# A memset of one unread column behind each gather on GpSimd (four graph layers on a sparse adjacency)

## The chip, the cores and the metric

The kernel runs on one core of a Trainium2 chip. The metric is device time in microseconds of one execution, as the median of three timed runs. A profile is one more execution of the same program with the hardware profiler on; its times are shown beside the timed runs and are not the same thing.

## What is computed

Four layers run one after the other on 4096 nodes with 128 features. Each normalises its input, applies ReLU, and adds the layer's result to its input. The adjacency matrix `adj` (4096 x 4096, float32) is mostly zeros, and the share of non-zeros falls from the first nodes to the last.

```python
h = relu(layernorm(x));  x = x + h @ W_self.T + (adj @ h) @ W_neigh.T + b          # layer 0
h = relu(layernorm(x));  T1 = adj @ h;  T2 = 2 * (adj @ T1) - h                     # layer 1
x = x + h @ w[0] + T1 @ w[1] + T2 @ w[2] + bias
h = relu(layernorm(x));  H = h @ weight.T                                           # layer 2: attention
C = (H * att_src).sum(-1)[None, :] + (H * att_dst).sum(-1)[:, None]
Tau = adj.T * exp(maximum(0.2 * C, C))
x = x + (adj.T * Tau / Tau.sum(1, keepdims=True)) @ H
h = relu(layernorm(x));  s = h @ msg_s;  d = h @ msg_d                              # layer 3: messages
agg[i] = sum_j gelu(s[i] + d[j] + msg_b) * adj[i, j]
x = x + layernorm(gelu(concat(h, agg) @ upd.T + upd_b) + h) * ln_w + ln_b
```

## The kernel before

**Dense part and lists.** The nodes are reordered on the host so that the well-connected ones come first. Products with `adj` are done in stripes of 256 rows or columns (`ROWS`, `COLS`). For each stripe the near blocks of 128 nodes (the first ones and its own) are read and multiplied whole. For the rest the kernel makes a list on the chip of the (node, stripe) pairs that hold a non-zero, and fetches only those: a piece of 256 values of `adj` and the node's feature row, 128 list entries in one gather. For layer 3 it makes a list of the single non-zero entries (`entries`), with their column numbers (`e_col`), addresses (`e_at`) and values (`e_val`). If a list should overflow, a branch at the end runs a dense fallback (`dense_stack`); it is not run with these inputs.

**The gathers.** Every gather goes through one helper, `gather`, at line 552: an indirect DMA issued by GpSimd that takes 128 row numbers from a column in SBUF and fetches these rows of a table in DRAM. It is called from six places:

- `Layer.gather`: for layers 0 to 2 of the products (layer 1 is two of them), the pieces of `adjT` (`rseg`, only in the first product, from where SP stores them to `r_tab` for the later ones) and the feature rows (`g` from `h_tab` and `u_tab`)
- `fetch_columns`: the pieces of `adj` by column (`cseg`), which SP stores to `c_tab` for the attention layer
- `Attention.rows`: rows of `a_tab` (`g`)
- `values`: the values `e_val`, 4 bytes for each partition
- `Messages.rows`: rows of `d_tab`, into the message buffers (`m`, and later the halves of the attention buffers, which the trace calls `tau` and `e`)

**The order.** A planner (`Plan`) runs when the program is built. Each piece of work is a generator that yields what it wants next: an event, a buffer, or an engine for some time. The planner takes them in order of the time at which they could begin and of their rank, and so writes out one fixed order of instructions for each engine; `in_order` then pins it. A gather is booked as `GATHER`, 1.27 us of GpSimd (`"POOL", 1.27`), and its data as landing 4 us after the transfer. The planner also puts matmuls of zeros (`fill`, line 610) into gaps of TensorE. Instructions that are issued without a `yield` cost nothing in the plan.

**What waits for what.** Buffers set the pace between the engines: 14 tiles `g` for feature rows, 6 `cseg`, 8 `rseg`, 4 messages at first and more later. A gather waits until the buffer's last reader is done (PE for `g`, SP's store for `rseg` and `cseg`), and PE waits until the gathered rows have landed. Dependencies between engines are semaphores: each engine has its own count, and DMAs from GpSimd and from SP have eight counts each, used in turn. GpSimd's other work is small: the constants at the start, and the bias additions at lines 980 and 1001.

Of the kernel before, what the change touches and what calls it, by code (L numbers as in the profile page):

```python
# [27 lines left out]
P = 128  # L28
# [350 lines left out]
def sparse_stack(tc, x, adj, adjT, diag, w_self, w_neigh, b0, w1, b1, w2, att_src, att_dst,  # L379
# [7 lines left out]
    nc = tc.nc  # L387
    plan = Plan()
    EARLY = 7
    with ExitStack() as ctx:  # L390
# [4 lines left out]
        def tiles(pool, name, n, shape, dtype=F32):  # L395
            return Slots([pool.tile(list(shape), dtype, name=f"{name}{i}", tag=f"{name}{i}") for i in range(n)])

        def kept(name, shape, dtype=F32):
            return keep.tile(list(shape), dtype, name=name, tag=name)
# [149 lines left out]
        junks = tiles(keep, "junk", 2, (P, D))  # L549
        aggs = tiles(keep, "agg", 2, (P, BANK))  # L550

        def gather(dst, table, index):
            nc.gpsimd.indirect_dma_start(out=dst, out_offset=None, in_=table[:, :],  # L553
                                         in_offset=bass.IndirectOffsetOnAxis(ap=index, axis=0))


        def norm(blocks, dst):
# [174 lines left out]
        def fetch_columns():  # L732
            for s in COLS:
                if s.cap:
                    yield col_list[s.index]
                for k in range(s.cap):
                    t = yield csegs
                    yield GATHER
                    gather(t, adj_segments, seg_col[:, s.chunk + k:s.chunk + k + 1])
                    here, left = Event(), Count(1)  # L740
                    here.set(plan.transfer(P * CS * 4))
                    plan.start(store(here, t, csegs, left, c_tab[s.index][k * P:(k + 1) * P, :], c_done[s.index],
                                     P * CS * 4), 6)
                    plan.start(give_back(left, csegs, t), 0)
# [186 lines left out]
        def values():  # L931
            for number, group in enumerate(GROUPS):
                yield decoded[number]
                for u in group.units:
                    for k in range(u.chunk, u.chunk + u.cap):
                        yield GATHER
                        n = u.within(k)
                        gather(e_val[:n, k:k + 1], adj_flat, e_at[:n, k:k + 1])
                        valued[u.number].set(plan.finish + plan.LANDING)
                    plan.start(valid(u), 7)  # L940
# [125 lines left out]
        class Layer:  # L1066
# [36 lines left out]
            def gather(self):  # L1103
                for s in ROWS:
                    if s.cap:
                        yield row_list[s.index]
                    for c in range(s.cap):
                        if self.number == 0:
                            t = yield rsegs
                            yield GATHER  # L1110
                            gather(t, adjT_segments, seg_row[:, s.chunk + c:s.chunk + c + 1])
                            here, left = Event(), Count(2)
                            here.set(plan.transfer(P * RS * 4))
                            self.at["seg", s.index, c] = t, here, left
                            plan.start(store(here, t, rsegs, left, r_tab[s.index][c * P:(c + 1) * P, :],
                                             r_done[s.index], P * RS * 4), 2)
                            plan.start(give_back(left, rsegs, t), 0)
                        g = yield rows_g
                        yield self.table_done
                        yield GATHER  # L1120
                        gather(g[:, :D], self.table, fetch_row[:, s.chunk + c:s.chunk + c + 1])
                        self.at["row", s.index, c] = g
                        self.rows_here[s.index][c].set(plan.transfer(P * D * 4))
# [538 lines left out]
def gnn_stack_kernel(tc, **args):  # L1662


    some_bad = sparse_stack(tc, **args)
    with tc.If(some_bad > 0):
        args.pop("diag")
        dense_stack(tc, **args)
# [329 lines left out]
```

## Time and profile before

| | before |
|---|---|
| median of three timed runs | 1174.64 us (1171.81 to 1176.21) |
| the profiled execution, its own time | 1485.49 us |
| its span | 1483.4 us |
| mean granted TensorE clock in it | 0.842 |
| gathers, all from line 553 | 736 |
| GpSimd busy with them | 727.74 us |
| traffic of SP's DMA queue | 186.45 MB |
| traffic of GpSimd's DMA queue | 48.27 MB |

The profiled execution took 311 us longer than the median of the timed runs. In the page and its views, PE is TensorE's matmuls, PEld its weight loads, DVE is VectorE, ACT ScalarE, POOL GpSimd and SP SyncE; an engine with a q behind it is that engine's sequencer, where DMAs are issued. A row of the timeline is: start in us from the span's start, duration in us, engine, line, operation, what it writes and reads, how many instructions are merged, and in brackets how long the engine had been idle and what ended that. "remote" and "another core or an unknown queue" mean that a semaphore was raised by something for which the profile has no matching instruction; "issue" means that the engine waited for nothing that the profile shows. A row of the waits is: engine, what waited, its line, what it waited for, and then total us, how often, and the longest.

Where the gathers lie, from the stretches of the profile (us from the start of the span):

| stretch | gathers | mean DMA share | what runs |
|---|---|---|---|
| 0 to 85 | 1 | 0.90 | first reading of `adj`, constants |
| 85 to 375 | 132 | 0.86 | rest of the reading, layer 0 |
| 375 to 900 | 304 | 0.54 | two products of layer 1, lists and values |
| 900 to 1200 | 164 | 0.34 | attention |
| 1200 to 1430 | 136 | 0.21 | messages |
| 1430 to 1484 | 2 | 0.09 | last blocks |

### The profile page before, as it was taken

What the parts mean: (1) busy time and instruction counts of PE and PEld (TensorE: products, weight loads), DVE (VectorE), ACT (ScalarE), POOL (GpSimd) and SP (SyncE); (2) the same over time, 40 slices, a digit from 0 to 9 for tenths busy, and PEclk for the clock granted to TensorE, in tenths of its full rate; (3) what the DMA queues carried; (4) which work ended last, traced back from release to release, by engine and by line L of the source; (5) the groups of instructions that cost most, each with busy time, mean ns of one, the idle gap of its engine ahead of it and who ended that gap; (6) DMA issues with size and microseconds to landing.
All of it is one profiled execution on the core that took longest, in us unless ns stands there. A gap on an engine that the chain in (4) does not pass through costs nothing.

```text
span 1483.4 us, 19188 instructions
## 1 busy us (share of the span) xinstructions
PE 1055.1 (71%) x5943; PEld 722.2 (49%) x5943; DVE 792.7 (53%) x2982; ACT 671.2 (45%) x1344; POOL 766.4 (52%) x832
## 2 busy tenths in 40 slices
PE   6786778877486687667677069968767872957774
PEld 2454556554265465455555045534434452645663
DVE  5796567787466476345645048444444451424453
ACT  5983466664021213113335048656555630334366
POOL 4136664344635565546656733765557346664530
PEclk9897799897697899778888579979888995988988
DMA  8999899895565777766544034333333212112210
GB/s 252 357 329 334 286 299 330 305 353 185 135 185 147 211 228 227 201 187 181 150 115 132 8 93 132 107 88 89 88 107 97 61 50 49 42 42 53 61 45 24
DMA packets 175415, 236.03 MB, mean 159 GB/s; under 512 B 22452, under 2 KB 155336, under 8 KB 167112
## 3 DMA queue, kind: packets, MB, share of 16 engines
q1 hardware_dynamic: 148904, 186.45, 37.8%
q0 software_dynamic: 26400, 48.27, 13.6%
q8 instruction: 49, 0.80, 0.2%
q14 instruction: 62, 0.51, 0.1%
HBM read 203.41 MB, written 31.23 MB: 158 GB/s over the span
## 4 chain that ended last, share of the span: by engine, by line
PE 23%; another core or an unknown queue 13%; ACT 10%; DVE 7%; issue 6%; DMA 1%; POOL 0%; ACTq 0%; SPq 0%; DVEq 0%; POOLq 0%
PE acc L1253 4%; PE acc L1255 3%; PE bank L597 2%; PE acc L1421 2%; PE acc L1139 2%; PE acc L1156 2%; ACT junk L1453 1%; ACT e L1229 1%; ACT junk L568 1%; PE bank L1411 1%; PE pick L610 1%; ACT e L1232 1%; PE bank L1409 1%; DVE ehit L891 1%
## 5 line engine op out<-in xcount | busy, mean ns | idle before, releaser
L553 POOL DMA_INDIRECT e_val<-in_adj,e_at x158 | 154.5, 978 | 48.0 <-issue 45.6
L553 POOL DMA_INDIRECT g<-h_tab,fetch_row x136 | 136.1, 1001 | 73.0 <-issue 34.3
L610 PE MATMUL pick<-nothing 128*128 128x512 f16 x536 | 142.9, 416 | 1.6 <-issue 1.6
L1139 PE MATMUL acc<-big,hA 128*128 128x256 f32 x448 | 131.7, 442 | 10.7 <-issue 7.7
L610 PEld LDWEIGHTS <-nothing 128*128 128x128 f16 x795 | 82.9, 107 | 99.3 <-issue 33.4
L553 POOL DMA_INDIRECT g<-a_tab,fetch_col x74 | 76.9, 1039 | 93.6 <-issue 45.3
L553 POOL DMA_INDIRECT rseg<-in_adjT,seg_row x68 | 71.1, 1046 | 103.4 <-issue 28.8
L1139 PEld LDWEIGHTS acc<-big,hA 128*128 128x128 f32 x448 | 96.4, 225 | 28.6 <-issue 9.5
L553 POOL DMA_INDIRECT cseg<-in_adj,seg_col x74 | 70.8, 957 | 63.9 <-issue 23.2
L891 DVE SCALAR_TENSOR_TENSOR ehit<-ehit,pos,pick 128x32 f32<-128x32 f32 (+7 forms) x158 | 38.8, 285 | 116.0 <-issue 80.1
L1236 DVE TENSOR_TENSOR tau<-e,big 128x512 f32<-128x512 f32 (+3 forms) x61 | 54.3, 891 | 85.5 <-ACT e L1232 47.8
L553 POOL DMA_INDIRECT g<-u_tab,fetch_row x68 | 64.6, 950 | 64.9 <-PE acc L1156 37.1
L888 ACT COPY ehit<-pick 128x192 f32<-128x192 f32 (+7 forms) x74 | 20.4, 286 | 154.5 <-remote 80.4
L553 POOL DMA_INDIRECT tau<-d_tab,e_col x63 | 60.6, 962 | 57.2 <-issue 15.0
L769 ACT ACTIVATE mask<-dst 128x2048 fp8e4<-128x2048 f32 x43 | 81.8, 1903 | 14.2 <-DMA dst<-in_adj 8.0
L553 POOL DMA_INDIRECT m<-d_tab,e_col x70 | 68.4, 977 | 38.5 <-issue 17.4
L1156 PE MATMUL acc<-big,g 128*128 128x256 f32 x272 | 80.2, 434 | 0.6 <-DMA big<-r_tab 0.5
L568 ACT ACTIVATE junk<-xN,stat 128x128 f32<-128x128 f32 x128 | 51.4, 401 | 60.0 <-DVE stat L564 27.0
L623 ACT ACTIVATE sel_t<-iota_row,mids 128x512 f32<-128x512 f32 (+3 forms) x43 | 27.1, 642 | 109.7 <-DVE mids L618 63.7
L610 PE MATMUL bank<-nothing 128*128 128x512 f16 x259 | 70.6, 414 | 2.7 <-issue 2.3
L884 PE MATMUL pick<-eA,esel 128*128 128x65 f16 (+7 forms) x158 | 27.0, 245 | 61.4 <-DVE esel L625 28.0
L1139 PE MATMUL acc<-big,hB 128*128 128x256 f32 x224 | 62.7, 420 | 1.7 <-DMA big<-in_adjT 1.7
(331 smaller groups left out, 2717.2 us busy)
## 6 DMA issues: line engine op xcount, KB each, us to landing
dst<-in_adj SPq DMA_DIRECT2D x43, 1024.0 KB
big<-in_adjT SPq DMA_DIRECT2D x45, 512.0 KB
raw<-in_adj SPq DMA_DIRECT2D x21, 1024.0 KB
big<-in_adjT SPq DMA_DIRECT2D x66, 256.0 KB
big<-r_tab SPq DMA_DIRECT2D x30, 512.0 KB
c_tab<-cseg SPq DMA_DIRECT2D x74, 128.0 KB
r_tab<-rseg SPq DMA_DIRECT2D x68, 128.0 KB
big<-c_tab SPq DMA_DIRECT2D x15, 512.0 KB
```

What stands on the lines that cost most here:

```text
L553: nc.gpsimd.indirect_dma_start(out=dst, out_offset=None, in_=table[:, :], in_offset=bass.IndirectOffsetOnAxis(ap=index, axis=0))
L568: nc.scalar.activation(junk, src[:, k, :], AF.Square, bias=st[:, 0, k:k + 1], accum_out=st[:, 1, k:k + 1])
L597: nc.tensor.matmul(p[:, k * D:(k + 1) * D], lhs[:, k * P:(k + 1) * P], w, start=i == 0, stop=i == len(terms) - 1)
L610: nc.tensor.matmul(idle[2][idle[1]], nothing[:, :P], nothing, start=True, stop=True)
L769: nc.scalar.activation(mask[:, h * HALF:(h + 1) * HALF], raw_of[b, h], AF.Sigmoid, scale=1e38, accum_out=marks[:, 2 * b + h:2 * b + h + 1] ...
L891: nc.vector.scalar_tensor_tensor(hit[:, q, :], hit[:, q, :], pos0[:, k + q:k + q + 1], pv[:, q, W:2 * W], op0=ALU.is_le, op1=ALU.mult, acc ...
L1139: nc.tensor.matmul(acc, self.near[:, b, :D], as_rows(t)[:, k, :], start=count == 0, stop=count == every - 1)
L1156: nc.tensor.matmul(acc, row[:, :D], r, start=count == 0, stop=count == every - 1)
L1236: nc.vector.tensor_mul(tau[:, :n, :], e[:, :n, :], a[:, :n, :])
L1253: nc.tensor.matmul(acc[0:1, CS:2 * CS], parts[k][:, D + 1:], tau[:, k, :], start=False, stop=False)
L1255: nc.tensor.matmul(acc[:, :CS], parts[k][:, :D], e[:, k, :], start=False, stop=self.count[s.index] == every - 1)
L1421: nc.tensor.matmul(acc[:, b % GB * P:(b % GB + 1) * P], m[:, q, :], r[:, q, :], start=False, stop=all(self.left[g * GB + k] == 0 for k in ...
```

## The change

A tile of one column, 128 x 1 float32, is added, and `gather` writes zeros into it with a memset on GpSimd after each indirect DMA. Nothing reads this tile. The planner's booking of a gather is left as it is.

```diff
+        spacer = kept("spacer", (P, 1))
+
         def gather(dst, table, index):
+
             nc.gpsimd.indirect_dma_start(out=dst, out_offset=None, in_=table[:, :],
                                          in_offset=bass.IndirectOffsetOnAxis(ap=index, axis=0))
+            nc.gpsimd.memset(spacer, 0.0)
```

In the built program this is 736 memsets, each directly behind a gather on GpSimd's queue, and each with a wait on GpSimd's own count for the memset before it, since both write the same column.

## The prediction

> **What bounds the kernel now.** I read the times beside the page first, then the chain that ended last, then the waits of GpSimd, then stretches of the timeline in order of time.
>
> The first thing to see is that the profiled execution took 1485.49 us and the three timed ones have a median of 1174.64 us. So 311 us of the profile have no counterpart in the timed runs, and I have to find them before I use it. The page and its chain of waits:
>
> ```profile
> span 1483.4 us, 19188 instructions
> PE 1055.1 (71%) x5943; PEld 722.2 (49%) x5943; DVE 792.7 (53%) x2982; ACT 671.2 (45%) x1344; POOL 766.4 (52%) x832
> ...
> PE 23%; another core or an unknown queue 13%; ACT 10%; DVE 7%; issue 6%; DMA 1%; POOL 0%; ACTq 0%; SPq 0%; DVEq 0%; POOLq 0%
> ```
>
> No engine is full. 13% (13.4% by line, 199 us) of the chain is a wait with no visible releaser and 6.4% (95 us) is "issue". The long pieces are all of one kind. The timeline at the largest of them:
>
> ```profile
> 828.10 0.17 ACT L1042 ACTIVATE hB<-bank 128x2 f32<-128x2 f32 x1 [15.11 <-remote]
> 828.31 0.16 DVE L1044 COPY hB<-bank 128x2 f32<-128x2 f32 x1 [4.12 <-issue]
> ...
> 853.79 0.94 POOL L553 DMA_INDIRECT e_val<-in_adj,e_at  x1 [0.30 <-issue]
> 855.04 0.93 POOL L553 DMA_INDIRECT e_val<-in_adj,e_at  x1 [0.30 <-issue]
> 855.43 0.24 ACT L888 COPY ehit<-pick 128x96 f32<-128x96 f32 x1 [27.16 <-remote]
> 855.71 0.25 DVE L891 SCALAR_TENSOR_TENSOR ehit<-ehit,pos,pick 128x32 f32<-128x32 f32 x1 [26.91 <-issue]
> ```
>
> ACT waits 27.16 us for matmuls that, earlier in the timeline, started by 815.7 us. While every other engine stands still, GpSimd goes on gathering with 0.94 us busy and a 0.30 us gap. A similar wait of 32.43 us ends at 1258.5, again inside an unbroken run of gathers. Those two shares make 294 us, almost the 311 us that the timed runs do not have. My reading is that these standstills come mostly with being profiled, and that the timed runs are a program without them.
>
> What bounds that program is suggested by GpSimd's own waits:
>
> ```profile
> POOL g L553 <- issue: 93.7, 215, 28.9
> POOL g L553 <- PE acc L1156: 60.5, 20, 14.2
> ...
> POOL e_val L553 <- issue: 45.6, 150, 0.3
> POOL rseg L553 <- issue: 28.8, 47, 8.5
> POOL cseg L553 <- issue: 23.2, 65, 1.2
> ```
>
> Columns are total, times, longest. Adding m (57), tau (49) and e (19), 602 of the 736 gathers (82%) have no named releaser, mostly the plain 0.30 us: they follow another gather at once. A gather holds GpSimd for 1.25 us from start to start, not for its 0.94, so 736 of them are 920 us. Before 85 us there are none and after 1430 us two. Outside stand 85 + 54 = 139 us; if the timed run keeps those, 1175 - 139 = 1036 us are left for 920 us of gathers: 89% full. PE, DVE and ACT are below that in total. So GpSimd is close to the bound in the timed run, though the profile puts it at 52% and its share of the chain at 0%. The 89% is an upper reading: if profiling also stretches the gather itself, it is less.
>
> [...] The trace agrees that busy times mislead here: 128x1 memsets of 0.10 us start 0.03 us apart. [...]
>
> **The change part by part.** It removes nothing. It adds 736 memsets of 128x1, one behind each gather on GpSimd's queue, and one 4-byte column per partition. Set side by side, the two instruction streams differ in nothing else: outside the fallback branch PE, DVE, ACT and SP have the same instructions and waits in the same order, and no DMA is added or passes another. The planner doesn't know of the memset (it still books 1.27 us per gather).
>
> The memset carries one wait, on GpSimd's own count, for the memset before it (both write the same column). That one was issued a whole gather, 1.25 us, earlier and shows as 0.10 us long, so the wait should always be met. Queued behind it are the next gather and, eight times at line 1001, a bias addition; what waits for those is PE (gathered rows), SP (stores of segments) and DVE (values). Eight existing instructions lose a wait on the same count because the memset in front already covers it; I cost that at nothing.
>
> The price of one memset, from the trace:
>
> ```profile
> 0.28 0.10 POOL L1986 MEMSET const-float32-1.0<- 128x1 f32 x1
> ...
> 3.57 1.54 POOL L474 MEMSET unit_base<- 128x26 f32 x32
> 5.04 0.75 POOL L403 DMA_DIRECT2D b_sb<-in_b  x1
> ```
>
> 32 narrow memsets take from 3.57 to 5.04 us, so 0.046 us each. For the neighbours of a gather, the nearest rows are a bias addition between two gathers:
>
> ```profile
> 163.14 0.94 POOL L553 DMA_INDIRECT rseg<-in_adjT,seg_row  x1 [0.30 <-issue]
> 164.09 1.28 POOL L1001 TENSOR_TENSOR xN<-xN,b_sb 128x512 f32<-128x512 f32 x1
> 165.53 0.96 POOL L553 DMA_INDIRECT g<-h_tab,fetch_row  x1 [0.16 <-issue]
> ```
>
> It starts 0.01 us after the gather ends, and the gap before the next gather is 0.16 instead of 0.30: 0.14 us of its 1.28 overlap with the start of the gather. By this row a 0.10 us memset could cost nothing. Bounds: 0 below (all hidden), 0.10 us above (its whole busy time, nothing overlapped), and 0.26 us if 0.10 plus a 0.16 gap came on top of the 0.30. Below nothing only by the first rival. I take 0.046: 736 x 0.046 = 34 us of GpSimd's time.
>
> What of this lies on the path? None where DMA sets the pace: from 85 to 375 us DMA is 0.86 busy and 132 gathers x 1.25 fill 165 of 290 us, 57%. That leaves 604 gathers, 28 us. Of those I count most but not all, since GpSimd also sits behind PE (the 60.5 us above), which absorbs some. I take 24 us, 70% of the 34. The sum on the profile's own execution: 1485 + 24 = 1509 us; the standstills can move this by far more than 24 either way. Against the timed median: 1174.6 + 24 = 1199, forecast 1198.
>
> **The rivals.**
>
> Faster: the spacer breaks the standstills. Place: the unbroken runs of gathers, 801 to 857 and 1208 to 1253 us above all. For it: engines stand still exactly there, and a short instruction that is no gather may let the others through. Against it: the 311 us leave room for almost none of them in the timed run, and each gather already leaves 0.30 us. Price: if a third of the 199 us (66) exists unprofiled and all of it goes, less the 24, the gain is 42: 1132 us. It decides the sign once more than 24 us of real standstill is cured.
>
> No change: GpSimd has slack. For it: 0% of the chain and waits behind PE. It needs less than 6 us of the 34 on the path, under 18%: 1176 us. Against it: 82% of the gathers follow a gather.
>
> Much slower: the memset does not overlap. At 0.10 us, 74 us on GpSimd, 70% on the path 52: 1226 us. At 0.26, 191 and 134: 1308 us, which the 0.16 gap after the addition speaks against.
>
> **How the numbers follow.** Forecast 0.47 (its own range 1182 to 1215), faster rival 0.28, no change 0.12, much slower 0.13. A measurement of this kernel can tell about 0.5%, 6 us. So faster 0.28, same 0.12, slower 0.60. The range to hold 8 in 10 takes in the forecast, the no-change case, the part of the faster case that stops at 1132, and the 0.10 us case: 1132 to 1240. Left out are larger cures (0.13) and the 0.26 end (0.05).
>
> **What would show it.** GpSimd's start-to-start time of two gathers with a memset between them: 1.25 + 0.05 us is my step, 1.25 the no-change row, 1.35 or more the costly rival. The memset's idle before it should be about nothing; an idle that names GpSimd itself would prove the wait on its own count wrong. The wait with no named releaser should stay near 13% of the chain if the memset does not touch the standstills. If it shrinks to a few per cent and the timed median falls with it, the standstills were real and my reading of the 311 us is wrong; if it shrinks in the profile while the time rises, the reading holds and only the profile was cured. A time below 1169 us proves the forecast wrong outright.

## The result, and the profile after

The change makes the kernel slower by half a per cent: 1183.54 us (median of 19 runs, 1175.28 to 1187.99) against 1175.98 us for before (19 runs in the same comparison), ratio 1.0052, 95% interval 1.0035 to 1.0069. As a share of 1176 us that is about 6 us, 4 to 8 by the interval. The forecast was 24 us.

One thing has to be known to read the numbers: in some places (chips, or occasions: the record does not tell these apart) this program takes about 1176 us whether or not it is changed, and in others, profiled or not, 1477 to 1521 us, so each ratio is between runs of one comparison on one chip, with their slow executions left out, and is not the quotient of the two medians.

The page of the changed kernel, its first part, the chain of waits and, from the costliest groups, two of GpSimd's (busy us, mean ns of one, then idle time of the engine before them):

```profile
span 1184.9 us, 19920 instructions
PE 984.4 (83%) x5943; PEld 673.4 (57%) x5943; DVE 792.3 (67%) x2982; ACT 672.6 (57%) x1344; POOL 865.8 (73%) x1568
...
POOL 27%; PE 21%; DMA 19%; DVE 14%; ACT 11%; issue 7%; POOLq 0%; SPq 0%; DVEq 0%; ACTq 0%
...
L556 POOL DMA_INDIRECT e_val<-in_adj,e_at x158 | 158.9, 1006 | 30.0 <-issue 28.4
...
L558 POOL MEMSET spacer<- 128x1 f32 x736 | 94.6, 129 | 0.3
```

The instruction count is up by 732 (736 memsets, and four other records fewer), and PE, DVE and ACT have the counts of before. The chain now adds up to about 100% and has no wait without a releaser; GpSimd leads it with 27%. The 736 memsets show 94.6 us of busy time, but hardly any idle in front of them (0.3 us in all).

The next view is GpSimd's timeline in an unbroken row of gathers:

```profile
690.07 0.94 POOL L556 DMA_INDIRECT e_val<-in_adj,e_at  x1 [0.19 <-issue]
691.01 0.12 POOL L558 MEMSET spacer<- 128x1 f32 x1
691.32 0.94 POOL L556 DMA_INDIRECT e_val<-in_adj,e_at  x1 [0.19 <-issue]
692.26 0.11 POOL L558 MEMSET spacer<- 128x1 f32 x1
692.57 0.95 POOL L556 DMA_INDIRECT e_val<-in_adj,e_at  x1 [0.19 <-issue]
```

A gather starts every 1.25 us, as before the change. The 0.30 us that stood empty between two gathers now hold a memset of 0.12 us and a gap of 0.19. Over all start-to-start times below 1.7 us the median is 1.249 us here and 1.249 us in the profile of before. So the memset's busy time, 94.6 us by the page, is nowhere in the queue's pace. (The profile of before comes from one of the slower places; the start-to-start time was 1.249 or 1.250 us in all of them.)

It would be easy to read a 300 us gain into the two profiles, 1483.4 us against 1184.9 us. The timed runs beside them say +0.5%. That pair of profiles compares two places more than two kernels, and the first experiments had to separate the two.

### The profile page after: what moved, and what is told of

Same layout as the page of the kernel before. It is cut to its first block, busy times and chain, and to the rows that moved or that the text cites. A ratio compares the mean times of both kernels' runs of the same rounds, so it can differ in the third digit from the quotient of the medians.

```text
span 1184.9 us, 19920 instructions
## 1 busy us (share of the span) xinstructions
PE 984.4 (83%) x5943; PEld 673.4 (57%) x5943; DVE 792.3 (67%) x2982; ACT 672.6 (57%) x1344; POOL 865.8 (73%) x1568
## 4 chain that ended last, share of the span: by engine, by line
POOL 27%; PE 21%; DMA 19%; DVE 14%; ACT 11%; issue 7%; POOLq 0%; SPq 0%; DVEq 0%; ACTq 0%
POOL e_val L556 7%; POOL g L556 6%; DMA g<-h_tab,fetch_row 4%; POOL m L556 4%; PE acc L1160 4%; POOL spacer L558 3%; PE acc L1143 3%; PE pick L614 3%; DMA dst<-in_adj 2%; PE bank L601 2%; ACT junk L572 2%; DMA cseg<-in_adj,seg_col 2%; DMA g<-a_tab,fetch_col 2%; ACT mask L773 2%; POOL cseg L556 2%
## 5 line engine op out<-in xcount | busy, mean ns | idle before, releaser
L556 POOL DMA_INDIRECT e_val<-in_adj,e_at x158 | 158.9, 1006 | 30.0 <-issue 28.4
L1143 PE MATMUL acc<-big,hA 128*128 128x256 f32 x448 | 119.5, 412 | 8.3 <-DMA big<-in_adjT 5.9
L1143 PEld LDWEIGHTS acc<-big,hA 128*128 128x128 f32 x448 | 87.8, 205 | 22.9 <-DMA big<-in_adjT 7.7
L558 POOL MEMSET spacer<- 128x1 f32 x736 | 94.6, 129 | 0.3
L556 POOL DMA_INDIRECT g<-a_tab,fetch_col x74 | 78.5, 1061 | 16.0 <-issue 10.3
L1160 PE MATMUL acc<-big,g 128*128 128x256 f32 x272 | 75.4, 411 | 11.7 <-DMA g<-h_tab,fetch_row 6.6
L1143 PE MATMUL acc<-big,hB 128*128 128x256 f32 x224 | 59.6, 402 | 11.3 <-DMA big<-in_adjT 11.1
L614 PE MATMUL bank<-nothing 128*128 128x512 f16 x259 | 66.6, 399 | 0.0
L1160 PEld LDWEIGHTS acc<-big,g 128*128 128x128 f32 x272 | 51.6, 202 | 22.7 <-DMA g<-h_tab,fetch_row 8.7
```

Source lines behind the costliest of these rows:

```text
L558: nc.gpsimd.memset(spacer, 0.0)
L614: nc.tensor.matmul(idle[2][idle[1]], nothing[:, :P], nothing, start=True, stop=True)
L1143: nc.tensor.matmul(acc, self.near[:, b, :D], as_rows(t)[:, k, :], start=count == 0, stop=count == every - 1)
L1160: nc.tensor.matmul(acc, row[:, :D], r, start=count == 0, stop=count == every - 1)
```

## The experiments

In the tables and texts, "start-to-start" is the median distance of two gathers less than 1.7 us apart, and "standstill" is the sum of all stretches over 2 us in which PE, PEld, DVE and ACT start no instruction; both are counted from the trace. Medians in the tables are over all timed runs of an experiment. Experiments on one chip were e1 to e4, e5 to e8, e9 to e12, e13 to e16, and e17 with e18; on all five, before took 1477 to 1521 us.

### Do the standstills belong to the profile, and does the change cure them?

The kernel before was run again without an edit, three times (e1, e5, e9), and the change once (e6).

> The kernel before, unchanged, profiled and timed once more. Timed ratio to before 1.000 within 0.3%. Theory 'the standstills belong to a profiled kernel without the memset': its span is near 1480 us again, with 13% of the chain without a releaser. Rival 'the standstills were an accident of that one execution': its span is near 1176 us and the median start-to-start time of back-to-back gathers is still 1.249 us, GpSimd about 80% taken.

> The kernel before, unchanged, for a profile beside the next three. Ratio 1.000 within 0.4%. Theory 'the standstills go with the place where the program runs': its timed median and its profile agree, either both near 1176 us with no standstill or both near 1485 us with them. Rival 'the standstills go with the profile': timed near 1176 us and profiled near 1485 us. In both the start-to-start time of back-to-back gathers is 1.249 us.

> The kernel before once more, for its profile beside the next three. Ratio 1.000 within 0.4%. By the runs so far timed and profiled time agree on one chip: both near 1485 us or both near 1176 us. In the second case the profile shows what the change was measured against: start-to-start 1.249 us, GpSimd's gathers nearly one unbroken row from 100 to 1140 us, no wait without a releaser.

> The change, unchanged. Where before takes about 1176 us: ratio 1.003 to 1.007 and start-to-start 1.249 us, as measured. Where before takes about 1485 us: theory 'the memset is no cure for the standstills, its queue time is hidden': ratio 1.00 to 1.02 (the own-column memsets gave 1.0127, the pairs 1.0233); rival 'it cures them': ratio below 0.97.

| run | timed median, us | ratio to before (95%) | span of its profile, us | start-to-start, us | standstill, us |
|---|---|---|---|---|---|
| e1 before | 1484.65 | 0.9981 (0.994 to 1.0021) | 1493.8 | 1.249 | 162 |
| e5 before | 1480.08 | 1.0066 (1.0021 to 1.0111) | 1471.4 | 1.250 | 158 |
| e9 before | 1507.66 | 1.0017 (0.9956 to 1.0079) | 1502.4 | 1.249 | 170 |
| e6 change | 1498.89 | 1.0139 (1.0064 to 1.0214) | 1508.6 | 1.249 | 179 |

Timed and profiled runs agree on every chip. The long times are therefore not made by the profiler, and neither, it follows, are the standstills: they come and go with the place. e5 is the same kernel as its reference and still reads 1.0066, with an interval up to 1.0111, so in these places a ratio within about 1% of 1 says nothing.

The timeline of e9, at the same work that stood still in the profile of before:

```profile
866.50 0.94 POOL L553 DMA_INDIRECT e_val<-in_adj,e_at  x1 [0.30 <-issue]
867.75 0.92 POOL L553 DMA_INDIRECT e_val<-in_adj,e_at  x1 [0.30 <-issue]
868.80 0.24 ACT L888 COPY ehit<-pick 128x96 f32<-128x96 f32 x1 [27.17 <-remote]
...
869.08 0.25 DVE L891 SCALAR_TENSOR_TENSOR ehit<-ehit,pos,pick 128x32 f32<-128x32 f32 x1 [26.92 <-issue]
```

ACT waited 27.17 us, at the same instruction and for as long as in the profile of before (27.16). The change has such waits too when it runs in such a place; from e6's timeline of ACT:

```profile
848.01 0.24 ACT L892 COPY ehit<-pick 128x96 f32<-128x96 f32 x1 [16.04 <-remote]
850.11 0.58 ACT L1169 COPY agg<-acc 128x512 f32<-128x512 f32 x1 [1.86 <-remote]
867.93 0.17 ACT L1046 ACTIVATE hB<-bank 128x2 f32<-128x2 f32 x1 [17.24 <-remote]
```

So a memset of one column cures nothing, and the calm profile of the changed kernel was taken where, by the timed 1176 us of before, there was little to cure.

The changed kernel was thus profiled in both kinds of place, and its two traces can be set side by side. In the first 85 us, with one gather, they agree: 382 matmuls in the calm trace and 375 in e6, at a granted clock of 0.92 in both. Then e6 falls behind as the gathers go on, by 10 us at the 41st, 129 us at the 361st and 302 us at the last. Standstills of over 2 us are 179 us of that in e6 and 14 us in the calm trace; so they are about half of the difference, and the rest is shorter waits and longer matmuls (PE is busy 1061 us against 984 us). The granted clock of TensorE is lower in the slow places, 0.82 to 0.85 against 0.92 to 0.94, and could be a cause of its own. In the profile of before it is 0.50 inside the standstill from 812 to 856 us and 1.00 in busy work from 900 to 940 us. Whether the lower clock adds to the time by itself or only goes along with the standstills is not shown; no run separates the two.

### Is it the wait on GpSimd's own count, or the number of memsets?

e2 gives each memset a column of its own, which takes the wait away. e3 and e10 put two memsets behind each gather.

```diff
-        spacer = kept("spacer", (P, 1))
+        spacer = kept("spacer", (P, 736), U8)
+        used = iter(range(736))
-            nc.gpsimd.memset(spacer, 0.0)
+            k = next(used)
+            nc.gpsimd.memset(spacer[:, k:k + 1], 0)
```

```diff
-        spacer = kept("spacer", (P, 1))
+        spacers = [kept(f"spacer{i}", (P, 1)) for i in range(2)]
-            nc.gpsimd.memset(spacer, 0.0)
+            for spacer in spacers:
+                nc.gpsimd.memset(spacer, 0.0)
```

> Each memset writes a column (one byte per partition) of its own, so none waits on GpSimd's own count. Theory 'the memset lies in the 0.30 us that a gather leaves anyway, and the 6 us come from something else than the wait': ratio 1.003 to 1.007, as the change. Rival 'the 6 us are the wait on its own count': ratio 1.000 within 0.2%. In both the start-to-start time stays 1.25 us.

> Two memsets of 128x1 behind each gather, on two columns. Theory 'cover': the second adds about 0.03 to 0.05 us, because 0.12 us of memset and 0.19 us of gap already fill the 0.30 us: start-to-start 1.28 to 1.30 us, ratio 1.015 to 1.03 (736 x 0.04 = 29 us, most of it on the path as GpSimd is nearly full). Rival 'the price was always 0.046 us a memset and the path takes only a fifth of it': start-to-start also up, but ratio only 1.010 (another 6 us).

> Two memsets again; start-to-start 1.25 us, as measured. Where before takes about 1176 us: theory 'each memset costs a little at places where gathers are not back to back': ratio 1.008 to 1.012, twice the change's. Rival 'the change's 0.5% has nothing to do with the number of memsets': 1.003 to 1.007. Where before takes about 1485 us: 1.015 to 1.03.

e2 came to 1.0127 (1.0085 to 1.0168) with start-to-start 1.249 us, beside 1.0139 for the change on another chip. Both ratios that I had named for it, 1.000 and 1.003 to 1.007, failed. Nothing points to the wait as the price: without it the ratio is the same, and with it the memsets of the change stand idle for 0.3 us in all. A part of a per cent could still hide in these intervals. e3 gave 1.0233 (1.0171 to 1.0294) and e10 1.012 (1.0048 to 1.0191). My expectation that the second memset would add 0.03 to 0.05 us failed: start-to-start was 1.250 and 1.249 us. For e10 I had named 1.015 to 1.03 in such a place, and it fell just short. From e3's timeline of GpSimd:

```profile
641.78 0.14 POOL L559 MEMSET spacer<- 128x1 f32 x2
642.09 0.94 POOL L556 DMA_INDIRECT g<-u_tab,fetch_row  x1 [0.16 <-issue]
643.03 0.14 POOL L559 MEMSET spacer<- 128x1 f32 x2
643.33 0.94 POOL L556 DMA_INDIRECT g<-u_tab,fetch_row  x1 [0.16 <-issue]
```

Two memsets take 0.14 us and leave a gap of 0.16, again 0.30 together. The cover is not used up by one memset, nor by two. A median hides rare cases, so here are the means of the same distances. On e6's chip it is 1.273 us with one memset and 1.273 without (e5). On e3's chip it is 1.273 with e2's memset, 1.276 with two and 1.271 without (e1). On e10's chip it is 1.279 with two and 1.266 without (e9). Profiles of the kernel before differ by 0.007 us in this mean, so one memset shows nothing in it, and two show a hint of 0.005 to 0.013 us. In e3 and e10 the memsets also waited for GpSimd's own count, for 9.6 and 9.9 us in all. Whether the number of memsets matters for the time is inconclusive: e3 says more than the change, e10 says the same. All four runs with narrow memsets in these places read 1.2 to 2.3% above before, more than the 0.5% of the main comparison. After e5's 1.0066 that is a hint and no more, and what the time would go into is not shown.

### How long must the memset be to show?

The wider memsets were meant to measure the price: for 128x128 (e4) I expected 4 to 6% more time. It came out 3% faster, and the rest of the series follows that surprise. They are otherwise the change (`kept("spacer", (P, 128))`, `(P, 192)`, `(P, 2 * P)`, and `(P, 448), F16`). e12 puts one behind every second gather only, e16 writes 256 columns of the upper 64 partitions only.

e12:

```diff
-        spacer = kept("spacer", (P, 1))
+        spacer = kept("spacer", (P, 484), F16)
+        used = iter(range(736))
-            nc.gpsimd.memset(spacer, 0.0)
+            if next(used) % 2:
+                nc.gpsimd.memset(spacer, 0.0)
```

e16:

```diff
-        spacer = kept("spacer", (P, 1))
+        spacer = kept("spacer", (P, 2 * P))
-            nc.gpsimd.memset(spacer, 0.0)
+            nc.gpsimd.memset(spacer[64:128, :], 0.0)
```

> The memset is 128x128, about 0.20 us long by the rows of the kernel before. Theory 'cover, GpSimd nearly full': 0.20 + 0.19 us of gap against 0.30, so start-to-start 1.33 to 1.36 us, 59 to 80 us more on GpSimd, ratio 1.04 to 1.06 if 80% or more of it is on the path. Rival 'GpSimd has slack, a fifth is on the path': ratio 1.010 to 1.015 with the same start-to-start time.

> The 128x128 memset again (start-to-start 1.331 us, 0.082 us more than before, 60 us in all on GpSimd). Where before takes about 1176 us: theory 'GpSimd is nearly full': ratio 1.03 to 1.05; rival 'most of it falls in slack': 1.010 or less. Where before takes about 1485 us: again 0.96 to 0.98.

> The memset is 128x192, start-to-start about 1.385 us. Theory 'a sustained rate fills something, with a limit near 1.4 us a gather': between the two neighbours, ratio 0.91 to 0.95, standstills of over 2 us adding to 30 to 110 us. Rival 'the limit lies at or under 1.38': 0.87 to 0.90, better than 128x256, since less queue time is spent. Where before takes about 1176 us: 1.06 to 1.09.

> The memset is 128x256, about 0.33 us: start-to-start 1.44 us, 0.19 us more than before, 140 us in all on GpSimd. Where before takes about 1176 us: theory 'nearly full': ratio 1.08 to 1.11; rival 'slack': 1.03 or less. Where before takes about 1485 us: if what helps is the longer pause between gathers, ratio below that of 128x128 or equal to it; if that gain was chance, above 1.00.

> The 128x256 memset, start-to-start 1.438 us, 0.189 us more than before, 139 us in all on GpSimd. Where before takes about 1176 us: theory 'GpSimd nearly full, 70% or more of its queue time is on the path': ratio 1.08 to 1.12; rival 'slack, a fifth': 1.02 to 1.03. Where before takes about 1485 us: 0.89 to 0.91 again.

> The 128x256 memset as the base for the next one. Where before takes about 1485 us or more: 0.89 to 0.905; start-to-start 1.44 us.

> A memset of 128x448 half-precision columns behind every gather, start-to-start about 1.60 us, 0.16 us more than with 128x256, 118 us in all on GpSimd. With standstills gone in both, the difference in time over 118 us is the share of GpSimd's queue time on the path. Theory 'GpSimd nearly full': 80 to 118 us slower than the 128x256 memset. Rival 'a fifth is on the path': 20 to 30 us slower.

> A memset of 128x484 half-precision columns behind every second gather only: 0.38 us more behind every second one, the mean start-to-start is that of the 128x256 memset, 1.44 us. Where before takes about 1485 us: theory 'a sustained rate of gathers fills something, only the mean pace counts': ratio 0.88 to 0.92. Rival 'each gather needs a pause of its own': 0.95 or more. Where before takes about 1176 us: as the 128x256 memset, within 1%.

> The memset writes 256 columns of partitions 64 to 127 only. Theory 'a memset is hidden where it runs beside the preparation of the next gather on other partitions': start-to-start falls back to about 1.25 us and the ratio to 1.00 to 1.02. Rival 'the next gather waits for the whole memset whatever its partitions': start-to-start 1.44 us and ratio 0.89 to 0.91, as for all 128 partitions.

| memset | runs | start-to-start, us | ratio to before (95%) | standstill, us |
|---|---|---|---|---|
| none | e1, e5, e9 | 1.249 | 1 | 158 to 170 |
| 128x128 | e4 | 1.331 | 0.9696 (0.9625 to 0.9767) | 124 |
| 128x128 | e7 | 1.331 | 0.9813 (0.9726 to 0.99) | 132 |
| 128x192 | e15 | 1.388 | 0.919, 1397.44 / 1521.25, no interval (its four runs: 1374.53 to 1408.28) | 102 |
| 128x256 | e8 | 1.438 | 0.8966 (0.8868 to 0.9063) | 19 |
| 128x256 | e11 | 1.442 | 0.898 (0.8911 to 0.9049) | 33 |
| 128x256 | e13 | 1.438 | 0.892 (0.8854 to 0.8985) | 44 |
| 64x256 | e16 | 1.438 | 0.8923 (0.8857 to 0.8989) | 46 |
| 128x484 half precision, every second | e12 | mean 1.44 (1.26 and 1.63 in turn) | 0.9053 (0.8982 to 0.9125) | 53 |
| 128x448 half precision | e14 | 1.598 | 0.9358 (0.9284 to 0.9432) | 64 |

Two readings come out of this table. The first is the price. From the timelines of GpSimd in e4 and in e14:

```profile
639.49 0.95 POOL L556 DMA_INDIRECT g<-u_tab,fetch_row  x1 [0.16 <-issue]
640.43 0.22 POOL L558 MEMSET spacer<- 128x128 f32 x1
640.82 0.95 POOL L556 DMA_INDIRECT cseg<-in_adj,seg_col  x1 [0.16 <-issue]
```

```profile
704.72 0.49 POOL L558 MEMSET spacer<- 128x448 f16 x1
705.38 0.95 POOL L556 DMA_INDIRECT e_val<-in_adj,e_at  x1 [0.16 <-issue]
706.32 0.50 POOL L558 MEMSET spacer<- 128x448 f16 x1
```

In all of these rows the gap behind the memset is 0.16 us. In them and in the rows with one or two narrow memsets (gaps of 0.19 and 0.16 us behind 0.12 and 0.14 us of memset), a gather starts 0.30 us after the last one ended, or 0.16 us after the memset between them ended, whichever is later. So up to 0.14 us of memset cost nothing in pace, 0.22 us cost 0.08 (1.331 against 1.249), and 0.50 us cost 0.35. e16 speaks against the idea that it matters which partitions the memset writes: one of partitions 64 to 127 takes 0.33 us and leads to a start-to-start of 1.438 us, as one of all 128 does in e13. The preparation of a gather that its expectation names is not seen in any trace.

The second is the share of GpSimd's time on the path. e13 and e14 ran on one chip. e14 has 0.160 us more for each of 736 gathers, 118 us, and took 1418.95 instead of 1354.29 us, 65 us more, or 55%. My expectation named 80 to 118 us for a nearly full GpSimd and 20 to 30 for the rival; it fell between them. But the two differ in more than the pace, as their chains of waits show, e13 first:

```profile
PE 25%; POOL 20%; DVE 15%; issue 12%; DMA 12%; ACT 10%; another core or an unknown queue 5%; SPq 0%; POOLq 0%; ACTq 0%; DVEq 0%
```

```profile
POOL 42%; PE 20%; DMA 15%; issue 8%; DVE 8%; ACT 6%; SPq 1%; POOLq 0%; DVEq 0%; ACTq 0%
```

e13 still has 5% of unnamed waits (4.5% by line, 61 us) and e14 has none. What e14 saved there can hide as much of its longer queue, so 55% is more likely too low than too high, and nothing up to the whole 118 us is excluded. The clock differs too (0.86 against 0.89).

The table also shows that the standstills answer to pace. They shrink step by step as the gathers are spaced out, to 19 to 53 us at 1.44 us. At 1.598 us they are not shorter (64 us in e14, 44 and 46 us in e13 and e16 on the same chip), but e14 has no wait without a named releaser any more; its longest stretch, 10.7 us, ends when gathered values land. A pause behind every second gather does nearly as well as one behind each (0.9053 against 0.898 on the same chip), so a pause for each gather is not needed, which fits that the mean pace counts. A fixed number of gathers in a row does not bring a standstill on: the ten longest of e1 begin after 5 to 33 gathers less than 1.7 us apart, and in the calm trace of the change a row of 97 passes with one such stretch, of 4 us. The end of the standstills can be read in e8's chain of waits, where the share without a releaser is 1%:

```profile
PE 29%; POOL 27%; DVE 12%; DMA 12%; issue 9%; ACT 8%; another core or an unknown queue 1%; SPq 1%; POOLq 0%; ACTq 0%; DVEq 0%
```

Beside it e9, the kernel before:

```profile
PE 42%; DVE 16%; another core or an unknown queue 14%; issue 12%; ACT 10%; DMA 3%; POOL 1%; SPq 0%; ACTq 0%; DVEq 0%; POOLq 0%
```

With the unnamed waits nearly gone, GpSimd rises from 1% to 27% of the chain (20% in e13 and 24% in e11, where some are left). That it is the same 27% as in the calm profile of the change is chance, since e8's gathers are slower and its memsets longer.

### Does TensorE's filler matter, and can more be had?

e17 is the kernel before with the line `plan.filler = fill` taken out, so the 795 matmuls of zeros and their weight loads are not issued. e18 is the 128x256 memset with the planner's booking of a gather set to it.

```diff
-            plan.filler = fill
```

```diff
-GATHER = "POOL", 1.27
+GATHER = "POOL", 1.46
```

> The kernel before without the planner's filler: the matmuls of zeros at line 610, 795 of TensorE's 5943 matmuls with as many weight loads, are left out; nothing reads their result. Theory 'what fills up is shared by the instructions of all engines and by the gathers': standstills of over 2 us fall well below the 160 to 180 us of the kernel before, ratio 0.97 or less where before takes about 1485 us or more. Rival 'it is the gathers alone': standstills stay within 150 to 190 us and the ratio is 0.99 to 1.03.

> The 128x256 memset behind each gather, and the planner books 1.46 us for a gather instead of 1.27, so the order of instructions is made for the longer gather. Theory 'the order matters because GpSimd is nearly full': 0.86 to 0.885 against before (the pause alone gave 0.892 to 0.898). Rival 'the order is the same in effect': 0.885 to 0.91.

The expectations of e12, e15 and e17 speak of something that fills up; that is a picture and no run shows such a store. e17: 1.0162 (1.0073 to 1.025), standstill 194 us, start-to-start 1.250 us. About a seventh of TensorE's instructions less does not shorten the standstills, so there is no sign that their number brings these on. The time is no clean measure here, as the mean granted clock fell to 0.777 as well. e18: 0.9076 (0.8991 to 0.9161), start-to-start 1.440 us, standstill 23 us. The order made for longer gathers is no better than the pause alone (0.892 to 0.898 on other chips).

The versions with the 128x256 memset, without the new booking, take 10 to 11% less than before in the places where before takes 1477 us or more. Where before takes 1176 us they were not tried. An estimate from the two readings above: the memsets add 0.189 us x 736 = 139 us of queue time there, and with 55% to all of it on the path they should lose some 6 to 12%.

## Why the prediction was wrong

It forecast slower, by 24 us; slower was right, the size was four times too large. The sum was 736 x 0.046 us, of which 70% on the path.

**The price of one memset: this term failed.** I took 0.046 us from 32 memsets in a row at the start of the kernel. That is what a memset costs behind another memset. Behind a gather it falls into 0.30 us in which GpSimd starts nothing, and start-to-start stayed at 1.249 us with one (the change, e6) and 1.250 us with two (e3). The row with the bias addition said so before: a gap of 0.16 us instead of 0.30, hence 0.14 us of cover. The prediction read it, listed nothing as the lower bound, and still took the other row. The nearer row was the right one, because it was between two gathers. In place of 0.046 us the runs show 0.00 us at the median, and 0.002 us or less on the mean (e6 against e5, e2 against e1).

**The share on the path** was 70%, by judgement, and is not decided: e14 against e13 gives 55% at a slower pace, more likely too low than too high. With 55% to all on the path, the 4 to 8 us measured would be 0.005 to 0.020 us a memset. The pace of back-to-back gathers does not show that, so where these 6 us come from stays open. No run points to the wait on its own count (e2).

**GpSimd is nearly full in the undisturbed program**: right in what it counted, the time taken by the queue. In the profile of the change, gathers run from 101 to 1153 us, and 736 x 1.249 = 919 of these 1052 us are theirs, 87%; 89% was forecast. It leads the chain with 27%. So the no-change rival came close in size for another reason than it gave: the cover in front of each gather was enough, and slack of GpSimd was not needed.

**The wait is always met, and nothing else moves**: right. 0.3 us idle before 736 memsets, and the other engines' counts are the same.

**"These standstills come mostly with being profiled": wrong.** Timed and profiled runs agree in e1, e5 and e9, at 1480 to 1508 us timed and 1471 to 1502 us profiled. The sum that supported it, 294 us against 311 us, was a coincidence: it added all "issue" time of the chain to the unnamed waits, while the standstills counted from that trace are 174 us, and a slower place would have fitted as well. A timed run beside the profile on the same chip would have told; by these runs, the two I compared came from different places. The sign that the prediction had set for this came out the wrong way: the unnamed waits vanished from the profile while the time rose, which was to mean that only the profile had been cured. It did not allow for two places. The number took no harm, since the ratio asked for was measured where before takes 1176 us; that was luck.

**The faster rival**: a pause does shorten the standstills, but the change does not make one. In the slow places a pace of 1.44 us left 19 to 44 us of them and took about 10% off the time (ratios 0.892 to 0.898, e8, e11 and e13). One column does not lengthen the pace measurably (1.249 us in e6), for the same reason that it costs next to nothing.

## What to carry to other kernels

Price an added instruction between the neighbours it will have, by start-to-start times, and not by its busy time or by a row of its own kind: 94.6 us of busy memsets cost no pace here because each fell into an existing gap. A cheap pace is not yet a free change: the time still rose by 0.5%. When a profile and the timed runs differ by a quarter, run the same kernel timed and profiled on one chip before explaining the difference or comparing two profiles. Where engines stand still without a visible releaser while one queue runs on without pause, slow that queue down on purpose and see whether the time falls.

## What the runs showed of the hardware that was not expected

In some places all other engines stand still at times while gathers of 128 rows run back to back, one in 1.25 us: PE, DVE and ACT had standstills of 158 to 170 us in three profiles of the kernel before on three chips, with single waits of 27 us, while GpSimd kept its pace. Spacing the gathers to a mean of 1.44 us removed most of it and about 10% of the time, although it added 0.19 us to each gather; so the pace of the gathers has a part in it. In another place the same gathers at 1.249 us left only four stretches over 2 us, 14 us in all. What differs between the places, and by what way the gathers hold the others up, these runs do not show; leaving out TensorE's filler did not help. Between two gathers, 0.14 us of memsets (e3) left the median pace at 1.250 us, against 1.249 us without them (e1).
